# Two graph aggregations as one paired Strassen step in half PSUM banks, in a tuned two-layer GNN kernel

One core of one Trainium2 chip. The metric is the device time of the whole program in microseconds (us), the median of several runs. A profiled run also gives a span, about 1.8 us shorter than its time, and a trace.

## The reference, cut to what matters

64 graphs with 256 nodes and 512 features, everything fp32. Two layers, each followed by a residual and a layer norm:

```python
x   = jax.random.normal(..., (64, 256, 512))        # adj: (64, 256, 256), nodemask: (64, 256), all ones
# layer 0
deg = jnp.sum(adj, axis=-1, keepdims=True)
agg = jnp.einsum('bij,bjf->bif', adj, x) / jnp.maximum(deg, EPS)
out = jnp.einsum('bnf,of->bno', jnp.concatenate([x, agg], axis=2), W)
x   = layernorm(x + relu(out))
# layer 1
q, k = jnp.split(x @ Wqk, 2, axis=-1);  v = x @ Wv
agg  = jnp.einsum('bij,bjd->bid', adj, k * mask[:, :, None])
w    = inv_scale * mask * jnp.einsum('bid,bid->bi', q, agg)
x    = layernorm(x + softmax(w, axis=1)[:, :, None] * v)
```

## The kernel before

The kernel multiplies the weights first: layer 0 computes y = x W2 and then adj y; layer 1 computes x1 M with M = Wq Wk^T and takes its row-wise dot product with adj (mask x1). So each graph has two large products with weights (256 x 512 by 512 x 1024) and two aggregations (256 x 256 by 256 x 512). The large products already go by a Strassen step with seven block products (`product`); the aggregations go directly, four matmuls with 512 columns each. All accumulation is in PSUM: seven banks of 128 x 512 fp32 rotate (`bank`), and a block product often accumulates into the bank that ACT (the scalar engine) has just copied out, for example U -> copy -> U + S3\*T3 -> copy -> U + A22\*T4. I call that a *bank turn*.

```python
    def product(ps, a, b, start=True):
        for c in range(H):                                     # H = 2: two matmuls of 512 columns
            nc.tensor.matmul(ps, a[:, c, :], b[:, c, :], start=start and c == 0, stop=(c == H - 1),
                             skip_group_check=True)

    def aggregate(a, vals, t):                                 # goes
        ps = bank()
        for j in range(NT):                                    # NT = 2
            nc.tensor.matmul(ps, a[:, j, t * P:(t + 1) * P], vals[:, j, :],
                             start=(j == 0), stop=(j == NT - 1))
        return ps
    ...
    def transpose_rows(src, dst):                              # x1 -> x1T: 32x32 on DVE, the rest by 16 DMAs
        sq = pool.tile([P, P // Q, NF, NT, Q], F32, name="sq")
        for t in range(NT):
            nc.vector.transpose(sq[:, :, :, t, :].rearrange("p b c q -> p c b q"), src[:, t, :])
        to = dst.rearrange("f c (t a q) -> f (c t) a q", t=NT, q=Q)
        for a in range(P // Q):
            for b in range(P // Q):
                nc.sync.dma_start(to[b * Q:(b + 1) * Q, :, a, :], ...)
    ...
    def gather0(g):                                            # layer 0's aggregation, out of PSUM
        for t in range(NT):
            z = aggregate(adj_g, y, t)
            nc.vector.scalar_tensor_tensor(own[:, t, :], z, rdeg[:, t:t + 1], own[:, t, :],
                                           op0=OP.mult, op1=OP.add)
            nc.vector.scalar_tensor_tensor(own[:, t, :], own[:, t, :], 0.0, xg[:, t, :],
                                           op0=OP.max, op1=OP.add)
    def gather1(g):                                            # layer 1's, with a masked adjacency from GpSimd
        sums1[g] = row_sums(x1Ts.pop(g), nc.vector)
        for t in range(NT):
            nc.scalar.copy(agg[:, t, :], aggregate(adjm, x1s[g], t))
    ...
    for i in range(B + G + 2):                                 # layer 0 of graph i beside layer 1 of graph i-2
        if new: layer0_a(i)
        ... softmax of two graphs, in every second iteration ...
        if old: gather1(i - 2)
        if new: layer0_b(i)
        ...
        if old: layer1_a(i - 2)
        if new: gather0(i)
        if old: layer1_b(i - 2)
        if new: norm0(i)
        if i + 1 < B: prepare(i + 1)
```

## Time and profile before

| | before |
|---|---|
| time, median of 3 runs | 2049.61 us (2048.89 to 2050.76) |
| PE (matrix engine) busy | 2017.6 us of a span of 2047.8, 99% |
| DVE / ACT / POOL busy | 58% / 25% / 13% |
| first product of one graph to that of the next | 30.90 us, and 31.53 in graphs with a softmax |

A matmul with 512 fp32 columns is two records in the trace (the page counts x512 for the 256 matmuls of one aggregation). A line of the timeline joins like records that follow each other (x4 is one block product); its second column runs to the modelled end of the last one, so the distance between two starts is what a block product costs (1.72 us), not the duration (1.88). "[0.68 <-ACT y L205]" is idle time just before, and what ended it.

### The profile page before, as it was taken

To read this page: it belongs to the slowest core of one execution; us is meant where nothing else is said; L and a number is where in the kernel's file an instruction comes from. 1 tells how busy PE (TensorE), PEld (TensorE's weight loads), DVE (VectorE), ACT (ScalarE), POOL (GpSimd) and SP (SyncE) were. 2 spreads that over 40 slices of the span, in tenths; PEclk is the share of its full clock that TensorE was granted. 3 is DMA by queue.
4 is the path that set the end of the run, shared out by engine and by line. 5 is a ranking of instruction groups with operands and counts; after the bars stand their busy time and mean duration, and the time that the engine had idled before them with its cause. 6 is when DMAs were issued, how large, how long until landed. Compare 5 with 4: busy or idle time off the path is not lost.

```text
span 2047.8 us, 16517 instructions
## 1 busy us (share of the span) xinstructions
PE 2017.6 (99%) x4768; PEld 888.9 (43%) x4768; DVE 1188.1 (58%) x2729; ACT 521.3 (25%) x1094; POOL 273.3 (13%) x391
## 2 busy tenths in 40 slices
PE   7999999999999999999999999999999999999996
PEld 3444444444444444444444444444444444444442
DVE  3555656655556556566556565565665565655656
ACT  2222222222222222222222222222222222222122
POOL 4010111110110111111101101101111011011000
PEclk9999999999999999999999999999999999999998
DMA  7323332333232333333333323323333333223211
GB/s 244 99 70 84 91 82 75 95 77 88 82 88 79 85 91 86 81 76 94 77 90 87 91 72 86 91 85 80 77 93 82 87 90 82 67 77 77 56 37 52
DMA packets 384601, 174.22 MB, mean 85 GB/s; under 512 B 283776, under 2 KB 349440, under 8 KB 384512
## 3 DMA queue, kind: packets, MB, share of 16 engines
q1 hardware_dynamic: 382096, 167.92, 30.7%
q10 hardware_dynamic: 2144, 4.19, 0.6%
q8 instruction: 39, 0.64, 0.1%
q0 software_dynamic: 272, 1.05, 0.1%
q14 instruction: 50, 0.41, 0.1%
HBM read 105.97 MB, written 33.55 MB: 68 GB/s over the span
## 4 chain that ended last, share of the span: by engine, by line
PE 98%; DMA 1%; DVE 1%; ACT 0%; issue 0%; SPq 0%; DVEq 0%; ACTq 0%
PE mm L140 75%; PE mm L161 21%; DMA xT<-x_t 1%; DMA rows<-adj 0%; PE tp L295 0%; PE tp L281 0%; DMA wqk<-wqk_t 0%; DVE o L303 0%; DVE st L169 0%; DVE o L175 0%; DVE y L215 0%; ACT L287 0%; ACT y L205 0%; ACT rows L182 0%; DVE v L272 0%
## 5 line engine op out<-in xcount | busy, mean ns | idle before, releaser
L140 PE MATMUL mm<-w,s 128*128 128x512 f32 x1024 | 481.2, 592 | 0.0
L140 PE MATMUL mm<-t,s 128*128 128x512 f32 x1024 | 462.6, 594 | 5.1 <-ACT own L198 2.8
L140 PEld LDWEIGHTS mm<-t,s 128*128 128x128 f32 x1024 | 194.7, 190 | 250.7 <-issue 247.1
L140 PEld LDWEIGHTS mm<-w,s 128*128 128x128 f32 x1024 | 194.5, 190 | 245.0 <-issue 223.9
L188 POOL TENSOR_SCALAR adjm<-adj,mask_sb 128x256 f32<-128x256 f32 x128 | 65.7, 524 | 1483.4 <-PE mm L161 1322.5
L140 PE MATMUL mm<-w,x1T 128*128 128x512 f32 x512 | 243.7, 598 | 0.0
L140 PE MATMUL mm<-w,xT 128*128 128x512 f32 x512 | 240.6, 592 | 0.0
L161 PE MATMUL mm<-y,adj 128*128 128x512 f32 x512 | 230.4, 592 | 1.6 <-DVE y L215 1.6
L161 PE MATMUL mm<-x,adjm 128*128 128x512 f32 x512 | 230.4, 592 | 0.0
L215 DVE TENSOR_TENSOR y<-mm,y 128x512 f32<-128x512 f32 x64 | 44.3, 692 | 281.2 <-PE mm L140 281.2
L161 PEld LDWEIGHTS mm<-y,adj 128*128 128x128 f32 x512 | 97.1, 190 | 124.7 <-issue 106.9
L140 PEld LDWEIGHTS mm<-w,xT 128*128 128x128 f32 x512 | 97.5, 190 | 123.0 <-issue 118.5
L140 PEld LDWEIGHTS mm<-w,x1T 128*128 128x128 f32 x512 | 94.8, 190 | 108.6 <-issue 108.1
L161 PEld LDWEIGHTS mm<-x,adjm 128*128 128x128 f32 x512 | 94.9, 190 | 108.4 <-issue 106.7
L140 PE MATMUL mm<-t,xT 128*128 128x512 f32 x256 | 120.5, 593 | 1.4 <-ACT y L205 1.4
L140 PE MATMUL mm<-t,x1T 128*128 128x512 f32 x256 | 120.5, 593 | 0.7 <-ACT v L260 0.7
L303 DVE SCALAR_TENSOR_TENSOR o<-v,probs,x 128x512 f32<-128x512 f32 x128 | 119.0, 967 | 1.1
L182 ACT ACTIVATE rows<-rows 128x256 f32<-128x256 f32 x128 | 52.3, 409 | 257.1 <-DVE mv L170 166.2
L221 DVE SCALAR_TENSOR_TENSOR own<-mm,rdeg,own 128x512 f32<-128x512 f32 x128 | 95.0, 742 | 29.5 <-PE mm L161 29.5
L172 ACT ACTIVATE rstd<-mv,eps 128x2 f32<-128x2 f32 x128 | 37.4, 292 | 283.7 <-DVE mv L170 283.7
L257 DVE SCALAR_TENSOR_TENSOR agg<-mm,agg 128x512 f32<-128x512 f32 x64 | 44.0, 688 | 108.9 <-PE mm L140 108.8
L261 DVE TENSOR_TENSOR v<-mm,v 128x512 f32<-128x512 f32 x64 | 44.3, 691 | 90.8 <-ACT v L260 90.8
(68 smaller groups left out, 1802.8 us busy)
## 6 DMA issues: line engine op xcount, KB each, us to landing
xT<-x_t SPq DMA_DIRECT2D x64, 512.0 KB, 4.6
x<-x SPq DMA_DIRECT2D x64, 512.0 KB, 3.6
x1T<-sq SPq DMA_DIRECT2D x1024, 32.0 KB, 2.0
out<-o SPq DMA_DIRECT2D x64, 512.0 KB, 3.1
adj<-adj_t SPq DMA_DIRECT2D x64, 256.0 KB, 2.6
rows<-adj SPq DMA_DIRECT2D x64, 256.0 KB, 3.2
wqk<-wqk_t ACTq DMA_DIRECT2D x4, 512.0 KB, 11.1
w<-w_t ACTq DMA_DIRECT2D x2, 1024.0 KB, 9.1
```

Source lines behind the costliest of these rows:

```text
L140: nc.tensor.matmul(ps, a[:, c, :], b[:, c, :], start=start and c == 0, stop=(c == H - 1), skip_group_check=True)
L161: nc.tensor.matmul(ps, a[:, j, t * P:(t + 1) * P], vals[:, j, :], start=(j == 0), stop=(j == NT - 1))
L172: nc.scalar.activation(rstd, mv[:, :, 1], AF.Sqrt, bias=eps)
L182: nc.scalar.activation(r[:, t, :], r[:, t, :], AF.Copy, accum_out=deg[:, t:t + 1])
L188: nc.gpsimd.tensor_scalar(adjms[g][:, j, :], adjs[g][:, j, :], mask_sb[:, j, g:g + 1], 1.0, op0=OP.mult, op1=OP.mult)
L215: nc.vector.tensor_add(y[:, 0, :], p5, y[:, 0, :])
L221: nc.vector.scalar_tensor_tensor(own[:, t, :], z, rdeg[:, t:t + 1], own[:, t, :], op0=OP.mult, op1=OP.add)
L257: nc.vector.scalar_tensor_tensor(agg[:, 0, :], p2, 1.0, agg[:, 0, :], op0=OP.mult, op1=OP.mult, accum_out=sc[:, 0, at:at + 1])
L261: nc.vector.tensor_add(v[:, 1, :], p5, v[:, 1, :])
L303: nc.vector.scalar_tensor_tensor(o[:, t, :], v[:, t, :], p[:, t, g % G:g % G + 1], x1[:, t, :], op0=OP.mult, op1=OP.add)
```

## The change

The intent is to use seven block products in place of eight in the aggregations too. A 256 x 256 by 256 x 512 product has blocks with 256 columns only, so two aggregations share each PSUM bank: layer 0's of graph g in one half, layer 1's of graph g-1 in the other. The differences of the adjacency go to GpSimd, those of the values to DVE (the vector engine), the mask to two ACT copies. Layer 1's aggregation thereby moves one iteration earlier, and the iteration's end is interleaved: one product of layer 1, one pair of aggregation products, and so on.

```diff
-    def aggregate(a, vals, t): ...
     def prepare(g):
-        adjms[g] = ...                                          # masked adjacency, 2 x GpSimd
+        nc.gpsimd.tensor_add(sa[:, 0], a21, a22)
+        nc.gpsimd.tensor_sub(sa[:, 1], sa[:, 0], a11)
+        nc.gpsimd.tensor_sub(sa[:, 2], a11, a21)
+        nc.gpsimd.tensor_sub(sa[:, 3], a12, sa[:, 1])
+    def gather_a(g):
+        tv = pool.tile([P, 4, 2, HF], F32, name="tv", bufs=1)
+        nc.vector.tensor_sub(t1, b12, b11)
+        nc.vector.tensor_sub(t2, b22, t1)
+        nc.vector.tensor_sub(t3, b22, b12)
+        nc.vector.tensor_sub(t4, b21, t2)
+        def twice(ps, a, b, start=True):                         # HF = 256 columns each
+            for n, k in enumerate(which):
+                nc.tensor.matmul(ps[:, k * HF:(k + 1) * HF], sumsA[g - k][a], w[b][:, n, :],
+                                 start=start and n == 0, stop=True, skip_group_check=True)
+        def steps():
+            twice(u, "A11", "B11");  nc.scalar.copy(r11, of(u))
+            twice(p2, "A12", "B21"); nc.vector.tensor_add(r11, of(p2), r11)
+            yield
+            twice(p5, "S1", "T1")
+            twice(u, "S2", "T2", start=False); nc.scalar.copy(r12, of(u))
+            yield
+            twice(u, "S3", "T3", start=False); nc.scalar.copy(r22, of(u))
+            nc.vector.tensor_add(r22, of(p5), r22)
+            yield
+            twice(u, "A22", "T4", start=False); nc.scalar.copy(r21, of(u))
+            yield
+            twice(p5, "S4", "B22", start=False); nc.vector.tensor_add(r12, of(p5), r12)
+            yield
     def norm0(g):
         layer_norm(owns.pop(g), x1s[g])
+        for t in range(NT):                                      # masked x1: layer 1's half of the next step
+            nc.scalar.activation(values(g + 1)[:, 1, t, :], x1s[g][:, t, :], AF.Copy,
+                                 scale=mask_sb[:, t, g:g + 1])
-    layer1_a, layer1_b
+    def layer1_steps(g):        # the same seven products, a yield after each:
+        # A11*B11 | S1*T1 | S2*T2 | A12*B21 | S3*T3 | A22*T4 | S4*B22
     for i in range(B + G + 2):
...
-        if old: layer1_a(i - 2)
-        if new: gather0(i)
-        if old: layer1_b(i - 2)
+        z = gather_a(i) if i <= B else iter(())
+        step(l1, 2)
+        step(z); step(l1); step(z); step(l1); step(z); step(l1); step(z); step(l1); step(z)
```

Small edits come with it: Wv's load goes to another DMA queue, the buffer `sq` of the transposition is single, and the DMA scratch is smaller.

More of the change, by code (lines that the diff above doesn't have):

```diff
@@ L62, in resnorm_kernel @@
     NT, NF, NA = N // P, F // P, A // P
-    H = NF // 2
+    H, HF = NF // 2, F // 2
     assert NT == 2 and NF == 4
@@ L71, in resnorm_kernel @@
     ps_tp = ctx.enter_context(tc.tile_pool(name="ps_tp", bufs=1, space=bass.MemoryType.PSUM))
-    (xs, adjs, rows, xTs, sums0, adjms, rdegs, ys, owns, x1s, x1Ts, sums1, aggs, vs, scores, probs,
-     open0, open1) = ({} for _ in range(18))
+    (xs, adjs, rows, xTs, sums0, sumsA, rdegs, vals, owns, x1s, x1Ts, sums1, aggs, vs, scores, probs,
+     open0) = ({} for _ in range(17))
     def load(g):
@@ L100, in resnorm_kernel @@
         nc.sync.dma_start(mask_sb, mask_t)
-        nc.gpsimd.dma_start(w1[:, NF:, :], wv.rearrange("(c p) o -> p c o", p=P))
+        nc.sync.dma_start(w1[:, NF:, :], wv.rearrange("(c p) o -> p c o", p=P))
         ident = const.tile([P, P], F32, name="ident")
@@ L146, in transpose_rows @@
     def transpose_rows(src, dst):
-        sq = pool.tile([P, P // Q, NF, NT, Q], F32, name="sq")
+        sq = pool.tile([P, P // Q, NF, NT, Q], F32, name="sq", bufs=1)
         for t in range(NT):
@@ L156, in transpose_rows @@
                                   sq[a * Q:(a + 1) * Q, b].rearrange("p c t q -> p (c t) q"))
-    def aggregate(a, vals, t):
-        ps = bank()
-        for j in range(NT):
-            nc.tensor.matmul(ps, a[:, j, t * P:(t + 1) * P], vals[:, j, :],
-                             start=(j == 0), stop=(j == NT - 1))
-        return ps
     def layer_norm(src, dst):
@@ L185, in prepare @@
         nc.vector.reciprocal(rdegs[g], rdegs[g])
-        adjms[g] = pool.tile([P, NT, N], F32, name="adjm", bufs=4)
-        for j in range(NT):
-            nc.gpsimd.tensor_scalar(adjms[g][:, j, :], adjs[g][:, j, :], mask_sb[:, j, g:g + 1], 1.0,
-                                    op0=OP.mult, op1=OP.mult)
+        a, sa = adjs[g], pool.tile([P, 4, P], F32, name="sa", bufs=3)
+        a11, a21, a12, a22 = a[:, 0, :P], a[:, 0, P:], a[:, 1, :P], a[:, 1, P:]
+        nc.gpsimd.tensor_add(sa[:, 0], a21, a22)
+        nc.gpsimd.tensor_sub(sa[:, 1], sa[:, 0], a11)
+        nc.gpsimd.tensor_sub(sa[:, 2], a11, a21)
+        nc.gpsimd.tensor_sub(sa[:, 3], a12, sa[:, 1])
+        sumsA[g] = {"A11": a11, "A12": a12, "A22": a22, "S1": sa[:, 0], "S2": sa[:, 1], "S3": sa[:, 2],
+                    "S4": sa[:, 3]}
         sums0[g] = row_sums(xTs.pop(g), nc.gpsimd)
@@ L194, in layer0_a @@
         own = owns[g] = pool.tile([P, NT, F], F32, name="own")
-        y = ys[g] = pool.tile([P, NT, F], F32, name="y")
+        y = values(g)[:, 0]
         u, p5, p2 = bank(), bank(), bank()
@@ L209, in layer0_b @@
     def layer0_b(g):
-        s, w, own, y = sums0.pop(g), W0, owns[g], ys[g]
+        s, w, own, y = sums0.pop(g), W0, owns[g], values(g)[:, 0]
         u, p5 = open0.pop(g)
@@ L215, in layer0_b, with values, of @@
         nc.vector.tensor_add(y[:, 0, :], p5, y[:, 0, :])
-    def gather0(g):
-        own, y, adj_g, rdeg, xg = owns[g], ys.pop(g), adjs.pop(g), rdegs.pop(g), xs.pop(g)
+    def values(g):
+        if g not in vals:
+            vals[g] = pool.tile([P, 2, NT, F], F32, name="vals")
+        return vals[g]
+    def gather_a(g):
+        val = vals.pop(g)
+        which = [k for k in range(2) if 0 <= g - k < B]
+        k0, k1 = which[0], which[-1] + 1
+        b11, b12, b21, b22 = (val[:, k0:k1, t, h * HF:(h + 1) * HF] for t in range(NT) for h in range(2))
+        tv = pool.tile([P, 4, 2, HF], F32, name="tv", bufs=1)
+        t1, t2, t3, t4 = (tv[:, k, k0:k1, :] for k in range(4))
+        nc.vector.tensor_sub(t1, b12, b11)
+        nc.vector.tensor_sub(t2, b22, t1)
+        nc.vector.tensor_sub(t3, b22, b12)
+        nc.vector.tensor_sub(t4, b21, t2)
+        w = {"B11": b11, "B21": b21, "B22": b22, "T1": t1, "T2": t2, "T3": t3, "T4": t4}
+        zr = aggs[g] = pool.tile([P, 2, NT, F], F32, name="zr")
+        r11, r12, r21, r22 = (zr[:, k0:k1, t, h * HF:(h + 1) * HF] for t in range(NT) for h in range(2))
+        def twice(ps, a, b, start=True):
+            for n, k in enumerate(which):
+                nc.tensor.matmul(ps[:, k * HF:(k + 1) * HF], sumsA[g - k][a], w[b][:, n, :],
+                                 start=start and n == 0, stop=True, skip_group_check=True)
+        def of(ps):
+            return ps.rearrange("p (k f) -> p k f", k=2)[:, k0:k1, :]
+        def steps():
+            u, p5, p2 = bank(), bank(), bank()
+            twice(u, "A11", "B11")
+            nc.scalar.copy(r11, of(u))
+            twice(p2, "A12", "B21")
+            nc.vector.tensor_add(r11, of(p2), r11)
+            yield
+            twice(p5, "S1", "T1")
+            twice(u, "S2", "T2", start=False)
+            nc.scalar.copy(r12, of(u))
+            yield
+            twice(u, "S3", "T3", start=False)
+            nc.scalar.copy(r22, of(u))
+            nc.vector.tensor_add(r22, of(p5), r22)
+            yield
+            twice(u, "A22", "T4", start=False)
+            nc.scalar.copy(r21, of(u))
+            yield
+            twice(p5, "S4", "B22", start=False)
+            nc.vector.tensor_add(r12, of(p5), r12)
+            yield
+        return steps()
@@ L219, in gather0, with combine0 @@
+    def combine0(g):
+        own, z, rdeg, xg = owns[g], aggs[g][:, 0], rdegs.pop(g), xs.pop(g)
         for t in range(NT):
-            z = aggregate(adj_g, y, t)
-            nc.vector.scalar_tensor_tensor(own[:, t, :], z, rdeg[:, t:t + 1], own[:, t, :],
+            nc.vector.scalar_tensor_tensor(own[:, t, :], z[:, t, :], rdeg[:, t:t + 1], own[:, t, :],
                                            op0=OP.mult, op1=OP.add)
@@ L228, in norm0, with turn @@
         layer_norm(owns.pop(g), x1s[g])
+        for t in range(NT):
+            nc.scalar.activation(values(g + 1)[:, 1, t, :], x1s[g][:, t, :], AF.Copy,
+                                 scale=mask_sb[:, t, g:g + 1])
         x1Ts[g] = pool.tile([P, NF, N], F32, name="x1T")
         transpose_rows(x1s[g], x1Ts[g])
-    def gather1(g):
+    def turn(g):
         sums1[g] = row_sums(x1Ts.pop(g), nc.vector)
-        agg = aggs[g] = pool.tile([P, NT, F], F32, name="agg")
-        adjm = adjms.pop(g)
-        for t in range(NT):
-            nc.scalar.copy(agg[:, t, :], aggregate(adjm, x1s[g], t))
-    def layer1_a(g):
+    def layer1_steps(g):
         if g % G == 0:
@@ L244, in layer1_a, with dot @@
         at = g % G
-        s, w, agg = sums1[g], W1, aggs[g]
+        s, w, agg = sums1.pop(g), W1, aggs.pop(g + 1)[:, 1]
         v = vs[g] = late.tile([P, NT, F], F32, name="v", bufs=G + 2)
         q = pool.tile([P, F], F32, name="q")
-        u, p5, p2 = bank(), bank(), bank()
+        def dot(a, t, to):
+            nc.vector.scalar_tensor_tensor(q, a, 1.0, agg[:, t, :], op0=OP.mult, op1=OP.mult, accum_out=to)
+        u = bank()
         product(u, s["A11"], w["B11"])
         nc.scalar.copy(q, u)
+        dot(q, 0, part[:, at:at + 1])
+        yield
+        p5 = bank()
         product(p5, s["S1"], w["T1"])
-        nc.vector.scalar_tensor_tensor(q, q, 1.0, agg[:, 0, :], op0=OP.mult, op1=OP.mult,
-                                       accum_out=part[:, at:at + 1])
+        yield
         product(u, s["S2"], w["T2"], start=False)
         nc.scalar.copy(v[:, 0, :], u)
+        yield
+        p2 = bank()
         product(p2, s["A12"], w["B21"])
-        nc.vector.scalar_tensor_tensor(agg[:, 0, :], p2, 1.0, agg[:, 0, :], op0=OP.mult, op1=OP.mult,
-                                       accum_out=sc[:, 0, at:at + 1])
+        dot(p2, 0, sc[:, 0, at:at + 1])
+        yield
         product(u, s["S3"], w["T3"], start=False)
@@ L261, in layer1_a @@
         nc.vector.tensor_add(v[:, 1, :], p5, v[:, 1, :])
-        open1[g] = u, p5
-    def layer1_b(g):
-        s, w, agg, v = sums1.pop(g), W1, aggs.pop(g), vs[g]
-        sc, at = scores[g // G][0], g % G
-        u, p5 = open1.pop(g)
+        yield
         product(u, s["A22"], w["T4"], start=False)
-        nc.vector.scalar_tensor_tensor(agg[:, 1, :], u, 1.0, agg[:, 1, :], op0=OP.mult, op1=OP.mult,
-                                       accum_out=sc[:, 1, at:at + 1])
+        dot(u, 1, sc[:, 1, at:at + 1])
+        yield
         product(p5, s["S4"], w["B22"], start=False)
         nc.vector.tensor_add(v[:, 0, :], p5, v[:, 0, :])
+        yield
     def softmax_rows(k):
@@ L311, in resnorm_kernel, with step @@
     W1 = weight_sums(w1, "t1_")
+    def step(gen, n=1):
+        for _ in range(n):
+            next(gen, None)
     for i in range(B + G + 2):
-        new, old = i < B, 0 <= i - 2 < B
+        new = i < B
         if i + 2 < B:
@@ L321, in resnorm_kernel @@
             e = softmax_rows(k)
-        if old:
-            gather1(i - 2)
+        if 0 <= i - 2 < B:
+            turn(i - 2)
+        l1 = layer1_steps(i - 2) if 0 <= i - 2 < B else iter(())
+        step(l1)
         if new:
@@ L329, in resnorm_kernel @@
             finish(i - 2 - G)
-        if old:
-            layer1_a(i - 2)
+        z = gather_a(i) if i <= B else iter(())
+        step(l1, 2)
+        step(z)
+        step(l1)
+        step(z)
+        step(l1)
+        step(z)
+        step(l1)
+        step(z)
+        step(l1)
+        step(z)
         if new:
-            gather0(i)
-        if old:
-            layer1_b(i - 2)
-        if new:
+            combine0(i)
             norm0(i)
@@ L347 @@
     B, N, F = x.shape
-    nc = bacc.Bacc("TRN2", target_bir_lowering=False, num_devices=1)
+    nc = bacc.Bacc("TRN2", target_bir_lowering=False, num_devices=1, dynamic_dma_scratch_size=1024)
     given = {
```

## The prediction

> **What bounds the kernel now.** I read the page's busy line first, then the matrix engine's waits over the whole run, then one stretch of the steady state by windows, then the timeline for the distance between matmuls.
>
> ```profile
> PE 2017.6 (99%) x4768; PEld 888.9 (43%) x4768; DVE 1188.1 (58%) x2729; ACT 521.3 (25%) x1094; POOL 273.3 (13%) x391
> ...
> PE mm L140 75%; PE mm L161 21%; DMA xT<-x_t 1%; DMA rows<-adj 0%; PE tp L295 0%; PE tp L281 0%; DMA wqk<-wqk_t 0%; DVE o L303 0%; DVE st L169 0%; DVE o L175 0%; DVE y L215 0%; ACT L287 0%; ACT y L205 0%; ACT rows L182 0%; DVE v L272 0%
> ...
> L161 PE MATMUL mm<-y,adj 128*128 128x512 f32 x512 | 230.4, 592 | 1.6 <-DVE y L215 1.6
> L161 PE MATMUL mm<-x,adjm 128*128 128x512 f32 x512 | 230.4, 592 | 0.0
> ```
>
> The second line is the chain that ended last: 96% of it is matmuls, 21% the aggregations (line 161) that the change rewrites. A busy PE alone proves little, so its waits:
>
> ```profile
> PE mm L111 <- DMA wqk<-wqk_t: 6.1, 1, 6.1
> PE tp L295 <- DVE e L289: 3.6, 1, 3.6
> PE mm L140 <- ACT own L198: 2.8, 1, 2.8
> PE mm L140 <- DVE t L120: 2.3, 1, 2.3
> PE mm L161 <- DVE y L215: 1.6, 2, 0.8
> PE mm L140 <- ACT y L205: 1.4, 2, 0.7
> PE mm L140 <- ACT v L260: 0.7, 1, 0.7
> ```
>
> These are all of them: 18.5 us, each at most twice, so they belong to the start and the end. By windows, the 1600 us from 200 to 1800 have 1600.00 us of PE at a clock of 1.00. In the steady state the time is the count of matmul records times their pitch. The pitch is in the timeline (columns: start, duration):
>
> ```profile
> 969.27 1.88 PE L140 MATMUL mm<-w,xT 128*128 128x512 f32 x4
> 970.99 3.60 PE L140 MATMUL mm<-t,s 128*128 128x512 f32 x8
> ...
> 996.74 1.88 PE L140 MATMUL mm<-t,x1T 128*128 128x512 f32 x4
> ```
>
> From 969.27 to 996.74 lie 64 records in 27.47 us: 0.4292 us each[...]. The page counts 512 records for 256 matmuls of the program (four per graph), so a program matmul with 512 columns is two records, 0.858 us[...]. A graph has 36 such matmuls (14 for each Strassen product, 8 for the aggregations): 72 records, 30.9 us. That fits two graphs in 62.43 us, with a softmax of some 0.6 us in every second one.
>
> [...]This trace's weight-load records last 190 ns, but two loads without a long matmul to hide behind stand 0.11 us apart:
>
> ```profile
> 1008.75 0.38 PE L281 MATMUL tp<-ident,scores 128*2 128x128 f32 x2
> 1008.76 0.08 PEld L281 LDWEIGHTS tp<-ident,scores 128*2 128x2 f32 x1 [0.34 <-issue]
> 1008.87 0.30 PEld L161 LDWEIGHTS mm<-x,adjm 128*128 128x128 f32 x2
> ...
> 1008.97 3.60 PE L161 MATMUL mm<-x,adjm 128*128 128x512 f32 x8
> ```
>
> Two transpose records of 128 output columns take from 1008.75 to 1008.97, 0.11 each[...], and the aggregation follows at once, though its weights began to load only 0.10 us earlier. [...]the two-input line 303, which runs beside POOL's sums, takes 967 ns, line 223 of the same form 694.
>
> **The change part by part.**
> PE: out go 8 matmuls of 512 columns per graph, 16 records of 0.4292: 6.87 us. In come seven block products for two graphs, each of 256 columns into its half of a bank: 14 matmuls, 28 records.[...] The gain is 0.825 us per graph, times 64: **52.8 us**. The first and the last step, with one graph only, are two halves and change nothing in the count.[...]
> DVE: four differences from SBUF and three additions from PSUM of 512 elements are new; line 221 reads SBUF in place of PSUM. In the timeline independent operations of that size start 0.60 to 0.66 apart: 7 x 0.65 = 4.5 us per graph, on top of 1188/64 = 18.6. That is 23.1 of some 30.4 us, 76%: not a bound by the sum.
> ACT: four copies of 0.58 for two, and two masked copies[...]: +2.5 on 8.1 us, 35%.
> POOL: the masked adjacency (2 x 0.52) goes, four differences of 128 x 128 come (estimate 0.4 each, from 0.73 for 256 columns): even.
> DMA: the same bytes; Wv's load moves to another queue, before it is needed.
>
> **What could turn into a wait.** The scheduled order of PE in the new kernel is: five products of layer 0, the first of layer 1, two of layer 0, then products of layer 1 (1.72 us each) in turn with pairs of aggregation products (0.86). I laid the measured durations on it by hand, PE running without a gap, and asked for each semaphore whether its producer is done.
> The tightest is PSUM reuse. Layer 1's S3*T3 is copied out by ACT and the next product accumulates in the same bank; now only one aggregation pair (0.864) lies between them, before it was four matmuls (3.4). The start of this trace shows such a turn bare:
>
> ```profile
> 36.34 1.88 PE L140 MATMUL mm<-w,s 128*128 128x512 f32 x4
> 38.26 0.58 ACT L205 COPY y<-mm 128x512 f32<-128x512 f32 x1 [0.58 <-PE mm L140]
> 38.89 1.98 PE L140 MATMUL mm<-t,xT 128*128 128x512 f32 x4 [0.68 <-ACT y L205]
> ```
>
> PE's last column went in at 36.34 + 4 x 0.4292 = 38.06 and PE went on at 38.89: 0.83 us. It fits into 0.864 by 0.03. I allow 0.03 a graph: 2 us.
> The differences T1 to T4 wait behind the last layer norm on DVE in softmax iterations, with POOL's sums beside them; there T2 is done about 20.3 us into the iteration, and PE asks for it at 22.1. The layer norm's end, now after the last aggregation product, gives the masked x1 at about 8.6 of the next iteration; it is asked for at 17. The softmax weights' transposes have 1.1 us to spare. None of these should show.
> The start is even: in the first two graphs no layer 1 fills the waits, but the scheduler puts the next graph's first product between; I add 0.5.
> The end is not: x1 of the last graph now comes some 6 us later (the aggregation ends the iteration, it used to precede the last two products). Its transposition through 16 DMAs, issued in 10.4 us (timeline before), ends near 21.8 us after the previous iteration, while PE has work until about 17, waits for masks and T1 (1.5) included. So +6.3 us.
> Sum: 2049.6 - 52.8 + 2 + 0.5 + 6.3 = **2005.6**, say 2005: 2.2% faster.
>
> **The rivals.**
> (a) The short record costs more than its columns: weights or instruction supply pace it. For it: weight-load records of 190 ns leave 26 ns in 216, and no matmul with 128 stationary columns and fewer than 512 output columns is in this trace. Against it: the 0.11 us spacing above. If a record took 230 ns, 1792 of them would add 25 us: 2030, within 2%. At 245 the gain is gone.
> (b) DVE or ACT become the bound within the iteration although their sums are not[...]. For it: DVE at 76%, two finishing layer norms moved into every second iteration, POOL's contention. Against: 0.9 us or more of slack at each of the points but the bank turn. If I am off by 1 us at one point, 0.3 to 1 us in every second graph: 10 to 30 us, 2015 to 2035.
> (c) Everything hidden and the end cheaper than I think: 1997 to 2000.
>
> **Range and chances.** The gain of 52.8 is firm if the pitch is; 2% is 41.0, so some 12 us of new waits are allowed and I count 8.8. Errors are likelier upward. Range 1998 to 2016; faster by over 2%: 0.66, within 2%: 0.32, slower: 0.02.
>
> **What would show it.** Right: records of 256 columns start 0.216 apart; two graphs pass in 62.43 - 1.65 = 60.8 us; PE's waits in the steady state come to under 5 us, and a wait for the transposed x1 of about 4.5 appears at the end; DVE 72 to 78% busy. Wrong: a pitch above 0.22 (rival a); a wait that recurs 32 or 64 times, on T (DVE), on a copy of layer 1's bank (ACT), or on layer 0's bank behind the masked copies (rival b).

It had put a record with 256 columns at 215.8 ns, so the 28 new records of a graph at 6.04 us, against 6.87 for the 16 old ones: 0.825 us a graph and 52.8 in all. With that the sum came to 2049.6 - 52.8 + 2 + 0.5 + 6.3 = 2005.6 us. The pitch was measured afterwards, in the changed kernel: 215.8 ns. From the trace before alone an estimate is possible: 0.11 us for a record of 128 columns and 0.4292 for one of 512, on a straight line, give 0.216 for 256. One masked copy on ACT in the changed kernel took 0.71 us on average (line 281).

## More of the kernel before

Near the start there are a product behind a wait of 2.82 us and a bank turn. Near the end there is another bank turn (2012.60), and the last graph's transposed x1 is asked for; it is there already, so there is no wait in front of the last line:

```profile
31.14 3.65 PE L140 MATMUL mm<-t,s 128*128 128x512 f32 x4 [2.82 <-ACT own L198]
...
56.34 1.98 PE L140 MATMUL mm<-t,xT 128*128 128x512 f32 x4 [0.68 <-ACT y L205]
...
2012.60 1.96 PE L140 MATMUL mm<-t,x1T 128*128 128x512 f32 x4
...
2016.12 2.74 PE L161 MATMUL mm<-x,adjm 128*128 128x512 f32 x6
2018.69 1.88 PE L140 MATMUL mm<-w,x1T 128*128 128x512 f32 x4
```

## The result, and the profile after

| | before | after |
|---|---|---|
| time, median | 2049.3 us (4 runs) | **2012.62 us** (4 runs, 2011.77 to 2013.55) |
| ratio | 1 | 0.982 (95%: 0.9803 to 0.9837) |

A ratio is the mean time of one kernel's runs over the mean of the other's in the same rounds, so it is not quite the ratio of the medians. The gain is 36.7 us, 1.8%. That is within the predicted range (1998 to 2016) but 7.6 us above the predicted 2005, and on the other side of the 2% line from the class that I had held likeliest.

The page of the kernel after, with the lines that answer to those of before (L142 is `product`, L240 is `twice`):

```profile
PE 1973.9 (98%) x5536; PEld 1030.4 (51%) x5536; DVE 1523.6 (76%) x3184; ACT 673.2 (33%) x1354; POOL 419.0 (21%) x518
...
L142 PE MATMUL mm<-w,x1T 128*128 128x512 f32 x512 | 242.5, 596 | 4.1 <-DMA x1T<-sq 4.1
...
L240 PE MATMUL mm<-tv,sa 128*128 128x256 f32 x768 | 187.1, 379 | 0.0
```

PE lost 43.7 us of busy time and is still the bound; DVE rose from 58 to 76%. All of PE's waits:

```profile
PE mm L113 <- DMA wqk<-wqk_t: 6.2, 1, 6.2
PE mm L142 <- DMA x1T<-sq: 4.1, 1, 4.1
PE mm L142 <- ACT own L197: 3.8, 1, 3.8
PE tp L349 <- DVE e L343: 3.6, 1, 3.6
PE mm L142 <- ACT vals L204: 3.0, 3, 2.1
PE mm L240 <- DVE vals L214: 1.6, 2, 0.8
PE mm L142 <- ACT v L311: 0.7, 1, 0.7
PE mm L142 <- ACT v L318: 0.7, 1, 0.7
PE mm L142 <- ACT q L304: 0.6, 1, 0.6
PE mm L142 <- DVE t L122: 0.4, 1, 0.4
```

No wait recurs from graph to graph, and by windows PE is again busy for 1600.00 us of the 1600 from 200 to 1800. Only the wait for x1T is new in kind. But this view does not tell everything, as the steady state shows. The timeline of PE, with the start of graphs' layer 0 (`mm<-w,xT` before a `mm<-t,s` x8) in the last three lines:

```profile
1002.74 1.89 PE L240 MATMUL mm<-tv,sa 128*128 128x256 f32 x8
1004.47 1.88 PE L142 MATMUL mm<-w,s 128*128 128x512 f32 x4
1006.18 1.03 PE L240 MATMUL mm<-tv,sa 128*128 128x256 f32 x4
1007.05 1.96 PE L142 MATMUL mm<-t,x1T 128*128 128x512 f32 x4
1008.84 1.03 PE L240 MATMUL mm<-tv,adj 128*128 128x256 f32 x4
...
1012.28 1.88 PE L142 MATMUL mm<-w,xT 128*128 128x512 f32 x4
...
1042.44 1.88 PE L142 MATMUL mm<-w,xT 128*128 128x512 f32 x4
...
1073.22 1.88 PE L142 MATMUL mm<-w,xT 128*128 128x512 f32 x4
```

Eight records with 256 columns take from 1002.74 to 1004.47, 0.216 each: the pitch is as predicted (over all steady runs of eight, 1.727 us, 215.8 ns each). Two graphs take 60.94 us (1012.28 to 1073.22) where I had said 60.8. The missing 0.14 to 0.16 is in the fourth line: A22\*T4 of layer 1 takes 1.80 us to the next start and not 1.72, in every graph. It is the product behind the bank turn that I had called the tightest. ACT's and the weight loads' rows of the same moment in the timeline:

```profile
1006.38 0.58 ACT L318 COPY v<-mm 128x512 f32<-128x512 f32 x1 [1.13 <-PE mm L142]
...
1007.02 0.30 PEld L142 LDWEIGHTS mm<-t,x1T 128*128 128x128 f32 x2 [0.21 <-ACT v L318]
```

The copy ends at 1006.96, and only then, at 1007.02, the first weights of the next product load: 0.03 us before the matmul at 1007.05. The matmul is not late, so no wait is counted, but its weights are, and the product is 0.08 us longer.

The span in three sections, from the starts of the first product of graph 3 and of graph 63 in the traces (the end runs to the start of the last matmul; some 12 us of layer norm and output follow in every kernel):

| | start, to graph 3 | middle, 60 graphs | end, from graph 63 |
|---|---|---|---|
| before | 95.26 | 1872.88 | 67.63 |
| after | 98.18 | 1828.21 | 71.92 |
| difference | +2.92 | -44.67 | +4.29 |

The middle is 60 x 0.745 us: 0.825 saved by the records, 0.079 given back at the bank turn. Of the start, 1.37 us is work moved there (layer 1's aggregation comes a graph earlier) and 1.55 are waits. In the end there are 4.67 us fewer records (that work, and the Strassen gain), so 8.96 us are waits or slow records.

The start: T4 of graph 1 waits 2.10 us where the kernel before waited 0.68 for the same bank turn.

```profile
54.86 1.33 ACT L281 ACTIVATE vals<-x,mask_sb 128x512 f32<-128x512 f32 x2 [0.81 <-DVE x L170]
56.10 0.56 ACT L204 COPY vals<-mm 128x512 f32<-128x512 f32 x1
...
56.72 1.98 PE L142 MATMUL mm<-t,xT 128*128 128x512 f32 x4 [2.10 <-ACT vals L204]
```

On ACT the bank copy (L204) stands behind the new masked copies (L281), and these had waited for the layer norm.

The end, on PE and then by windows (columns: stretch; its length; busy time and count of PE, PEld, DVE, ACT, POOL; PEclk; DMA share; GB/s):

```profile
1973.57 0.59 PE L240 MATMUL mm<-vals,sa 128*128 128x256 f32 x2
1978.28 3.75 PE L142 MATMUL mm<-w,x1T 128*128 128x512 f32 x4 [4.11 <-DMA x1T<-sq]
1981.83 4.72 PE L142 MATMUL mm<-t,s 128*128 128x512 f32 x8
1986.38 1.88 PE L142 MATMUL mm<-w,x1T 128*128 128x512 f32 x4
```

```profile
1978.28:1981.83 3.55, 3.55 (x5) 1.48 (x5) 1.50 (x4) 0.00 (x0) 0.00 (x0) 0.50 0.67 246
1981.83:1986.38 4.55, 4.55 (x9) 1.96 (x8) 0.70 (x2) 0.58 (x1) 0.00 (x0) 0.75 0.00 0
```

The wait for the last x1T was predicted. What follows was not: the granted clock is 0.50, then 0.75 on average. One block product takes 3.55 us and not 1.72, the next two 4.55 and not 3.43: 2.95 us lost to the wait's aftermath. PE's last column before the gap went in at 1974.00 (two records of 0.2158 after 1973.57). By windows the clock was 1.00 up to 1977.24, still inside the gap, 0.50 for the 6.83 us from there to 1984.07, and 1.00 behind that, up to 1994.2. It had fallen once before in this trace: behind a wait of 3.77 us that ended at 30.50 it was 0.50 for the 3.42 us from 31.65 to 35.07. The kernel before shows the same thing near its start: the product at 31.14, behind its wait of 2.82 us, took 3.44 us and not 1.72, at a clock of 0.51:

```profile
31.14:34.58 3.44, 3.44 (x4) 1.38 (x5) 3.44 (x5) 1.61 (x8) 3.44 (x2) 0.51 0.50 152
```

Extra waits predicted and found, in us: start 0.5 and 1.55; bank turn 2 and 4.75; end 6.3 and 8.96; sum 8.8 and 15.3. With the records' 52.8, 52.8 - 15.3 = 37.5 us, and the two spans differ by 37.6 (2047.8 and 2010.2).

### The profile page after: what moved, and what is told of

Read it like the earlier page. It is cut to its first block, busy times and chain, and to the rows that moved or that the text cites. A ratio compares the mean times of both kernels' runs of the same rounds, so it can differ in the third digit from the quotient of the medians.

```text
span 2010.2 us, 19340 instructions
## 1 busy us (share of the span) xinstructions
PE 1973.9 (98%) x5536; PEld 1030.4 (51%) x5536; DVE 1523.6 (76%) x3184; ACT 673.2 (33%) x1354; POOL 419.0 (21%) x518
## 4 chain that ended last, share of the span: by engine, by line
PE 95%; DVE 1%; ACT 1%; SPq 0%; issue 0%; DMA 0%; DVEq 0%; ACTq 0%
PE mm L142 75%; PE mm L240 19%; SPq L157 0%; PE tp L349 0%; PE tp L335 0%; DVE st L164 0%; DVE o L357 0%; DVE own L272 0%; ACT L341 0%; ACT vals L281 0%; DMA x1T<-sq 0%; ACT rows L177 0%; DVE o L170 0%; DVE own L274 0%; DVE v L325 0%
## 5 line engine op out<-in xcount | busy, mean ns | idle before, releaser
L142 PE MATMUL mm<-w,s 128*128 128x512 f32 x1024 | 481.3, 592 | 0.7 <-ACT v L311 0.7
L142 PE MATMUL mm<-t,s 128*128 128x512 f32 x1024 | 466.2, 597 | 4.8 <-ACT own L197 3.8
L142 PEld LDWEIGHTS mm<-t,s 128*128 128x128 f32 x1024 | 192.3, 190 | 236.7 <-issue 215.5
L142 PEld LDWEIGHTS mm<-w,s 128*128 128x128 f32 x1024 | 194.4, 190 | 192.8 <-issue 163.2
L142 PE MATMUL mm<-w,x1T 128*128 128x512 f32 x512 | 242.5, 596 | 4.1 <-DMA x1T<-sq 4.1
L142 PE MATMUL mm<-w,xT 128*128 128x512 f32 x512 | 242.0, 594 | 0.0
L183 POOL TENSOR_TENSOR sa<-adj 128x128 f32<-128x128 f32 x64 | 47.1, 736 | 781.0 <-PE mm L240 774.3
L134 POOL TENSOR_TENSOR s<-xT 128x256 f32<-128x256 f32 x64 | 47.7, 745 | 703.6 <-PE mm L142 685.8
L240 PE MATMUL mm<-tv,sa 128*128 128x256 f32 x768 | 187.1, 379 | 0.0
L240 PEld LDWEIGHTS mm<-tv,sa 128*128 128x128 f32 x768 | 145.8, 190 | 74.6 <-issue 59.6
L142 PEld LDWEIGHTS mm<-w,xT 128*128 128x128 f32 x512 | 97.9, 191 | 95.8 <-issue 92.4
L272 DVE SCALAR_TENSOR_TENSOR own<-zr,rdeg,own 128x512 f32<-128x512 f32 x128 | 107.6, 841 | 44.4 <-ACT zr L262 44.4
L142 PEld LDWEIGHTS mm<-w,x1T 128*128 128x128 f32 x512 | 95.3, 191 | 86.1 <-issue 74.6
L300 DVE SCALAR_TENSOR_TENSOR q<-mm,zr 128x512 f32<-128x512 f32 x128 | 87.7, 685 | 66.1 <-PE mm L142 66.1
L311 ACT COPY v<-mm 128x512 f32<-128x512 f32 x64 | 37.4, 585 | 299.0 <-PE mm L142 299.0
L142 PE MATMUL mm<-t,x1T 128*128 128x512 f32 x256 | 125.5, 612 | 0.7 <-ACT v L318 0.7
L142 PE MATMUL mm<-t,xT 128*128 128x512 f32 x256 | 120.6, 593 | 3.0 <-ACT vals L204 3.0
L240 PE MATMUL mm<-vals,adj 128*128 128x256 f32 x512 | 121.3, 379 | 1.6 <-DVE vals L214 1.6
L240 PEld LDWEIGHTS mm<-vals,adj 128*128 128x128 f32 x512 | 97.1, 190 | 43.2 <-issue 21.5
L214 DVE TENSOR_TENSOR vals<-mm,vals 128x512 f32<-128x512 f32 x64 | 44.3, 692 | 91.8 <-PE mm L142 91.8
```

The costliest lines, as they stand in the source:

```text
L134: eng.tensor_add(s1, a21, a22)
L183: nc.gpsimd.tensor_add(sa[:, 0], a21, a22)
L214: nc.vector.tensor_add(y[:, 0, :], p5, y[:, 0, :])
L240: nc.tensor.matmul(ps[:, k * HF:(k + 1) * HF], sumsA[g - k][a], w[b][:, n, :], start=start and n == 0, stop=True, skip_group_check=True)
L272: nc.vector.scalar_tensor_tensor(own[:, t, :], z[:, t, :], rdeg[:, t:t + 1], own[:, t, :], op0=OP.mult, op1=OP.add)
L300: nc.vector.scalar_tensor_tensor(q, a, 1.0, agg[:, t, :], op0=OP.mult, op1=OP.mult, accum_out=to)
```

## The experiments

My theory: the records give what was predicted; 4.7 us are lost at layer 1's bank turn in the steady state and about 7 us at the last x1T (wait and half clock). The rivals: (b) DVE or ACT are so near to bounding the iteration that freed time comes back elsewhere; (d) the small edits or the pairing in half banks cost something by themselves; (e) the half clock is not a consequence of the idle time. All kernels gave correct results. Runs e1, e3, e4 and e8 shared a chip and runs of the kernel before (median 2049.47), and e2, e5, e6 and e7 others (2049.5).

| run | time, us | ratio to before | start | middle | end |
|---|---|---|---|---|---|
| before | 2049.3 | 1 | 95.26 | 1872.88 | 67.63 |
| after | 2012.62 | 0.982 | 98.18 | 1828.21 | 71.92 |
| e1_reorder | 2005.48 | 0.9787 | 98.05 | 1823.48 | 69.92 |
| e3_fill | 2011.50 | 0.9815 | 99.33 | 1828.20 | 70.17 |
| e8_pe_turn | 2006.66 | 0.9790 | 99.25 | 1828.21 | 65.58 |
| e2_two_queues | 2006.11 | 0.9791 | 98.21 | 1828.21 | 65.79 |
| e4_twice_T | 2045.43 | 0.9978 | 103.26 | 1860.94 | 69.02 |
| e5_classical | 2055.90 | 1.0033 | 101.03 | 1875.28 | 66.83 |
| e7_side_edits | 2048.96 | 0.9997 | 94.57 | 1872.88 | 67.64 |
| e6_both | 2001.18 | 0.9764 | 99.94 | 1823.48 | 64.78 |

The sections are of the one profiled run of each. The middle repeats to 0.01 us between kernels that share its code. The start does not: for kernels with the code of the changed one there it lies between 98.05 and 99.94, so differences below 2 us are read from middle and end alone. The clock differs there too. In the changed kernel it stood at half for 3.42 us (31.65 to 35.07, a mean of 0.83 over 30 to 40 us). In e3 and e8 the means are 0.98 and 0.97 over 20 to 30 us and 0.68 and 0.69 over 30 to 40, which makes 6.8 us at half in each, by my estimate. In e6, with 0.83 over 30 to 40, it fell once more: 0.94 over 40 to 60 and 0.99 over 60 to 100, where the changed kernel has 1.00 (both kernels have a longest wait for line 204's bank copy of 2.1 us).

### e1_reorder: more work between the copy and the turn

```diff
     # layer1_steps
-        p2 = bank(); product(p2, s["A12"], w["B21"]); dot(p2, 0, sc[:, 0, at:at + 1])
-        yield
         product(u, s["S3"], w["T3"], start=False)
         ...
         product(u, s["A22"], w["T4"], start=False)
         dot(u, 1, sc[:, 1, at:at + 1])
         yield
+        p2 = bank(); product(p2, s["A12"], w["B21"]); dot(p2, 0, sc[:, 0, at:at + 1])
+        yield
```

A12\*B21, which has a bank of its own, moves behind A22\*T4; so S3\*T3 and A22\*T4 now have eight short records between them (1.73 us) and not four (0.86).

> Only the order of layer 1's products changes: S3*T3, then two aggregation pairs, then A22*T4, and A12*B21 moves behind it, so that 1.73 us of other matmuls (before 0.86) lie between the two that share a PSUM bank. Theory (the copy out of the bank ends 0.03 to 0.1 us too late, so the weight load of A22*T4 cannot be hidden): in the changed kernel A22*T4 takes 1.796 us to the next product in place of 1.717, in every graph; that 0.079 goes, two graphs take 60.78 us in place of 60.94, and the time falls by 5 us, from 2012.6 to about 2007.6. Rival (the 0.08 us is a cost of going from 256 columns back to 512, or of that operand): it stays with A22*T4 wherever it stands, and the time stays within 1 us.

Measured: 2005.48 us (2005.0 to 2006.57), ratio 0.9787 (0.9774 to 0.9801), 7.1 us under the changed kernel. Its timeline:

```profile
1944.03 1.89 PE L240 MATMUL mm<-tv,sa 128*128 128x256 f32 x8
1945.76 1.88 PE L142 MATMUL mm<-t,x1T 128*128 128x512 f32 x4
```

A22\*T4 (the second line) lasts 1.88 and not 1.96, 1.72 us to the next start, two graphs 60.78, and the middle is 4.73 us shorter: the bank turn is shown to be the loss of the steady state, all of it. The end gained 2.0 us as well: one turn fewer waits there (0.68), the softmax's transposition waits 3.3 and not 3.6, and after the same wait for x1T (4.04 us) the half clock lasted about 3.4 us and not 6.83, so the two products after it took 3.44 and not 4.55. I take that part for timing and not for the edit's doing, but no run shows what decides it. By windows the clock here was 1.00 up to 1973.36, where PE went on, 0.51 over the 3.48 us of the first product and 1.00 over the next 3.44; in the changed kernel PE went on at 1978.28, 1.04 us after the clock had fallen.

### e3_fill: keep PE busy during the last wait, with matmuls that nobody reads

```diff
+        if i == B:
+            fill = bank()
+            for _ in range(4):
+                nc.tensor.matmul(fill, aggs[B][:, 1, 1, :P], W1["B22"][:, 0, :], start=True, stop=True)
         if new:
             combine0(i)
```

> Four matmuls whose result nobody uses are put on PE before the last graph's layer 1, into the 4.1 us in which PE waits for the transposed x1. They do not make the data come sooner. Theory[...]: the wait shrinks to about 0.7 us but the first product of the last graph starts at the same time after its predecessor as before, at a clock of 1.00 in place of 0.50; its first two products take 1.72 us each, not 3.5 and 2.8: the time falls by 2.5 to 3 us, to about 2010. Rival (the two products are slow because they wait for row sums and DMA bytes): no change, 2012 to 2013.

(What it rested on is the end of the changed kernel: a wait of 4.11 us, and then a clock of 0.50 over one product and 0.75 over the next two.)

Measured: 2011.50 us (2011.3 to 2011.69), ratio 0.9815: 1.1 us under the changed kernel, less than the 2.5 to 3 that I had expected.

```profile
1974.72 0.59 PE L240 MATMUL mm<-vals,sa 128*128 128x256 f32 x2
1975.15 3.60 PE L404 MATMUL mm<-w,zr 128*128 128x512 f32 x8
1980.59 1.95 PE L142 MATMUL mm<-w,x1T 128*128 128x512 f32 x4 [1.84 <-issue]
1982.38 3.60 PE L142 MATMUL mm<-t,s 128*128 128x512 f32 x8
```

It went as thought: behind an idle stretch of 1.84 us the products run at full speed, 1.79 and 3.43 us, and by windows the clock is 1.00 from 1970 to 1987. So the half clock goes with the longer idle stretch, and rival (e) falls. The size was not as thought: from the end of the last aggregation product to the first product with x1T this kernel needs 5.44 us (1975.15 to 1980.59), the changed kernel 4.28 (1974.00 to 1978.28). In this run the sixteen DMAs took 11.47 us to issue and not 10.42; whether the fill caused that or it was chance, one profile doesn't tell. That 1.05 us, and a start that was 1.15 us longer, account for the shortfall.

### e8_pe_turn: the last graph's x1 transposed by PE, not by 16 DMAs

```diff
+    def turn_last(g):
+        for t in range(NT):
+            ps = bank()
+            for c in range(NF):
+                nc.tensor.transpose(ps[:, c * P:(c + 1) * P], x1s[g][:, t, c * P:(c + 1) * P], ident)
+            nc.vector.tensor_copy(x1Ts[g][:, :, t * P:(t + 1) * P], ps.rearrange("p (c n) -> p c n", c=NF))
     # norm0: transpose_rows only if g < B - 1;  main loop, before the last step(l1), step(z):
+        if i == B:
+            turn_last(B - 1)
```

> The last graph's x1 alone is transposed on PE (8 transposes, copied out by DVE) in place of VectorE's 32x32 blocks and 16 DMAs. Theory (the end's loss is a wait of 4.1 us for the 16 DMAs, and the granted clock that falls to 0.50 after it costs another 2.5 to 3): the wait for x1T and the half clock go, 8 transposes of 0.22 us come: the time falls by about 5 us, to 2007.5. Rival (the end is bound by the layer norm and the masked copies of the last graph, and the DMAs were hidden behind that): less than 1.5 us.

Measured: 2006.66 us (2005.73 to 2006.92), ratio 0.9790 (0.9777 to 0.9804), 6.0 us under the changed kernel.

```profile
1972.93 1.04 PE L291 MATMUL mm<-ident,x 128*128 128x128 f32 x8
1973.80 1.88 PE L142 MATMUL mm<-w,s 128*128 128x512 f32 x4
1975.52 0.59 PE L240 MATMUL mm<-vals,sa 128*128 128x256 f32 x2
1975.95 1.88 PE L142 MATMUL mm<-w,x1T 128*128 128x512 f32 x4
```

Eight transposes cost 0.87 us of PE (0.11 each, half of what I had expected), the product follows the aggregation without a gap, and the end is 6.34 us shorter: 4.1 of wait and 2.95 of half clock, less the transposes' 0.87, make 6.2. The middle is unchanged.

### e2_two_queues: the same 16 DMAs from two queues

```diff
-    def transpose_rows(src, dst):
+    def transpose_rows(src, dst, last=False):
...
-                nc.sync.dma_start(to[b * Q:(b + 1) * Q, :, a, :],
+                eng = nc.scalar if last and b % 2 else nc.sync
+                eng.dma_start(to[b * Q:(b + 1) * Q, :, a, :],
```

> For the last graph only, half of the 16 transposing DMAs are issued from the ACT queue. Theory (the end waits because one queue takes 10.4 us to issue them, 0.65 each): issued in some 5.2 us, x1T is there about 5 us sooner, but ACT's copies of the last aggregation stand behind its 8 issues; the wait of 4.1 us for x1T goes, about 2 us of waits for ACT come, the half clock does not: the time falls by 3 to 5 us, to 2008 to 2010. Rival (the transfers themselves or the completion take the time): the 16 land no sooner, and the time stays at 2012 or rises.

Measured: 2006.11 us (2005.75 to 2007.57), ratio 0.9791 (0.9778 to 0.9805), 6.5 us under the changed kernel. The timeline of its end, the issue of the DMAs on both queues first:

```profile
1966.21 5.19 SPq L158 DMA_DIRECT2D x1T<-sq  x8
...
1966.38 5.37 ACTq L158 DMA_DIRECT2D x1T<-sq  x8
...
1975.43 0.70 PE L241 MATMUL mm<-vals,sa 128*128 128x256 f32 x2
1975.97 1.02 PE L142 MATMUL mm<-w,x1T 128*128 128x512 f32 x2
1976.83 3.60 PE L142 MATMUL mm<-t,s 128*128 128x512 f32 x8
```

Two queues issue their eight DMAs side by side in 5.2 and 5.4 us, one queue issued its sixteen in 10.42. There is no wait for x1T and no half clock, and the gain is more than the 3 to 5 us expected. So it was the serial issue on one queue, not the transfers themselves, that made x1T late. In its place the waits show 0.5 us for a copy of the aggregation's bank (line 256): ACT, busy issuing until 1971.75, is late with its copies. PE does not notice more than that.

### e4_twice_T: the four new DVE differences computed twice

```diff
-        nc.vector.tensor_sub(t1, b12, b11)
-        nc.vector.tensor_sub(t2, b22, t1)
-        nc.vector.tensor_sub(t3, b22, b12)
-        nc.vector.tensor_sub(t4, b21, t2)
+        for _ in range(2):
+            nc.vector.tensor_sub(t1, b12, b11)
+            nc.vector.tensor_sub(t2, b22, t1)
+            nc.vector.tensor_sub(t3, b22, b12)
+            nc.vector.tensor_sub(t4, b21, t2)
```

This tests rival (b): how far is DVE from bounding the iteration?

> The four differences T1 to T4 are computed twice, so that DVE has 2.6 us more per graph (4.5 where POOL runs beside it) and is about 84% busy. Theory (DVE's part of the change is hidden, with 2.4 us of slack before PE asks for T2 in the graphs with a softmax and 3.8 in the others): nothing or at most 1 us in every second graph, 2012 to 2035. Rival (DVE is nearly the bound and the added 4.7 us per graph already show): its whole 2.6 us per graph comes through, 2150 or more.

Measured: 2045.43 us (2042.78 to 2046.88), ratio 0.9978, so 32.8 us slower than the changed kernel. Its waits and its timeline:

```profile
PE mm L241 <- DVE tv L231: 16.2, 33, 1.8
...
PE mm L241 <- DVE tv L232: 4.9, 30, 0.2
```

```profile
1023.90 1.10 PE L241 MATMUL mm<-tv,sa 128*128 128x256 f32 x4 [0.31 <-DVE tv L231]
1025.16 1.10 PE L241 MATMUL mm<-tv,sa 128*128 128x256 f32 x4 [0.16 <-DVE tv L232]
```

Both lines of the timeline are in a graph with a softmax. Such graphs took 31.88 us on average and not 30.78, the others 30.16 as in the changed kernel. So four more operations (some 2.5 us: their starts are 0.57 to 0.73 apart where POOL is idle) vanish in every second graph, and cost 1.09 us in the others. The step per graph was about what I had written, but the total that I put beside it was mis-multiplied: 1 us in every second graph is 32 us, which is 2045 and not the 2012 to 2035 of the text. The changed kernel has slack on DVE in graphs with a softmax, some 1.4 us by this sum (2.5 less 1.09), and in its own trace T2 is done 2.2 us (1.8 to 2.4) before PE starts on it, 3.7 in the other graphs. T never makes PE wait. Rival (b) is false for this kernel, though not far away.

### e5_classical: paired in half banks, but eight block products

```diff
+            for out, rows_, cols in ((r11, ("A11", "A12"), ("B11", "B21")), (r12, ("A11", "A12"), ("B12", "B22")),
+                                     (r22, ("A21", "A22"), ("B12", "B22")), (r21, ("A21", "A22"), ("B11", "B21"))):
+                ps = bank()
+                twice(ps, rows_[0], cols[0])
+                twice(ps, rows_[1], cols[1], start=False)
+                nc.scalar.copy(out, of(ps))
+                yield
```

No sums of the adjacency, no differences of the values, no accumulation over a copied bank in the aggregation; everything else is the changed kernel.

> The aggregations stay paired, half a bank each, with 256 columns, but as the 8 block products of the plain form: no differences of the adjacency or of the values, no additions after. It separates the eighth product from the way the pair is built. Theory (the time is the count of records times their pitch): 32 records of 0.2158 per graph, 6.91 us, 0.86 above the Strassen step and 0.04 above before; no stall at A22*T4, since 1.73 us lie between: two graphs in 62.5 us; with the end's wait 2056 to 2063, so 45 to 50 us above the changed kernel and slower than before by up to 0.7%. Rival (pairing or the interleaving itself gives or takes something in the steady state): two graphs differ from 62.5 us by over 0.2.

Measured: 2055.90 us (2055.84 to 2056.79), ratio 1.0033 (1.002 to 1.0045), just under the 2056 to 2063 expected. Two graphs take 62.51 us.

```profile
1937.86 1.89 PE L228 MATMUL mm<-vals,adj 128*128 128x256 f32 x8
1939.59 1.88 PE L142 MATMUL mm<-t,x1T 128*128 128x512 f32 x4
1941.30 1.89 PE L228 MATMUL mm<-vals,adj 128*128 128x256 f32 x8
```

Per graph it is 31.255 us: 0.040 more than before, as 32 x 0.2158 (6.906) against 16 x 0.4292 (6.867) says; and 0.785 more than the changed kernel, as four records (0.863) less the bank turn's 0.079 say. (Here eight records lie in the turn, and A22\*T4 takes 1.71.) So in the steady state pairing in half banks costs nothing but these 0.040 us, and the whole gain of the change is the eighth of the block products that Strassen's step leaves out. The profiled spans of e5 and before differ by 7.2 us: 2.4 of it in the middle, 5.8 at the start, to which a whole aggregation (3.45) is moved, and the end gives back only 0.8. I read that as the price of the shifted aggregation at the edges and not of the half banks; no run shows it apart.

### e7_side_edits: the kernel before with the three small edits alone

```diff
-        nc.gpsimd.dma_start(w1[:, NF:, :], wv.rearrange("(c p) o -> p c o", p=P))
+        nc.sync.dma_start(w1[:, NF:, :], wv.rearrange("(c p) o -> p c o", p=P))
-        sq = pool.tile([P, P // Q, NF, NT, Q], F32, name="sq")
+        sq = pool.tile([P, P // Q, NF, NT, Q], F32, name="sq", bufs=1)
-    nc = bacc.Bacc("TRN2", target_bir_lowering=False, num_devices=1)
+    nc = bacc.Bacc("TRN2", target_bir_lowering=False, num_devices=1, dynamic_dma_scratch_size=1024)
```

> The kernel before with only the change's side edits: Wv loaded on the sync queue in place of GpSimd's, one buffer for the transposition's squares in place of two, the smaller scratch for dynamic DMA. Theory (they make room and cost nothing): 2049.5 within 1.5 us, two graphs in 62.43. Rival (they have a part in the start's 1.5 us): 1.5 to 3 us more, all of it before graph 3.

Measured: 2048.96 us (2048.71 to 2049.11), ratio 0.9997 (0.9985 to 1.001): the same. With e5, rival (d) falls: neither the edits nor, in the steady state, the pairing cost anything that matters.

### e6_both: e1 and e8 together

The edit is the sum of the two diffs.

> The two changes that worked alone, together: layer 1's products reordered (alone 2005.5, of which 61 x 0.079 = 4.8 us in the steady state) and the last graph's x1 transposed on PE (alone 2006.7). Theory (they touch different places and add up): 2012.6 - 4.8 - 6.5 = 2001, 2.3 to 2.4% below before; two graphs in 60.78 us, no wait for x1T, no half clock between graph 3 and the final softmax. Rival (the reorder already took part of the end's loss, 7.1 us in all for 4.8 in the steady state): 2002 to 2004.

Measured: **2001.18 us** (1999.74 to 2001.83), ratio 0.9764 (0.975 to 0.9777): the fastest of all, 2.4% under the kernel before, and the one whose interval lies wholly beyond 2%. The middle is that of e1, the end is shorter still than that of e8. In middle and end it gains 11.87 us on the changed kernel (4.73 + 7.14), and e1 and e8 apart 13.07 (6.73 + 6.34): the half clock that was some 3.4 us shorter in e1 is gone altogether in e8 (1.00 from 1975 to 1992), so that part cannot be had twice.

## Why the prediction was right or wrong

- **The records (52.8 us): right.** Pitch 215.8 ns where 215.8 was predicted; the weight-load records of 190 ns did not pace it (rival a). The middle gives 60 x 0.824 once the bank turn is taken out.
- **The bank turn (0.03 a graph, 2 us): the place right, the size wrong.** It is 0.079 a graph, 4.75 us in sixty graphs; e1 gave all of it back. The step that failed is "0.83 us. It fits into 0.864 by 0.03". I measured the turn at the start of the matmul (38.89) and overlooked the same row's duration, 1.98 where a product without a turn has 1.88: the first weights load only after the copy, and that lengthens the product by another 0.10. So the turn needs about 0.93 us, 0.07 more than it has. The case itself stood in the before kernel's trace: its last graph's A22\*T4 (2012.60) comes two records, 0.86 us, after S3\*T3, lasts 1.96 and takes 1.80 to the next start.
- **DVE and ACT (rival b): right.** DVE 76% as worked out, ACT 33% (35%), no recurring wait. T2 is done 2.2 us before PE starts on it in softmax graphs, where I had 1.8.
- **POOL ("even"): wrong, without effect.** It went from 273 to 419 us. The differences took 0.45 to 0.78 us each on average, not 0.4, and the longer feature sums rose too (one from 725 to 1116 ns, while DVE's busy share rose from 58 to 76%). Off the path.
- **The start (0.5): too small.** 1.55 us of waits, nearly all of it one: ACT's bank copy behind the masked copies, 1.4 us more than before. I had looked at the scheduled order of PE, and for the start not at ACT's. The other 1.37 us of the longer start is work that the end no longer has, so it costs nothing by itself. No experiment took this wait away.
- **The end (6.3): the waits right, their aftermath missing.** Waits that the kernel before does not have there sum to 5.38 us (4.11 for x1T where I had 4.5 to 4.8, 0.68 and 0.59 behind ACT), and about 0.6 more is left by subtraction; weights exposed behind the two ACT waits (0.1 each, as above) can be part of it. The 2.95 us that failed is the half clock after the gap. The prediction treated a wait as costing its own length; e3 and e8 show that this one also slowed the next three products. This too could have been read beforehand, from the before kernel's product at 31.14: 3.65 us in the duration column, where 1.88 is usual.
- **The chances.** Of the 12 us of new waits that the 2% line allowed I had counted 8.8, with errors "likelier upward"; 15.3 came. The three terms missed by +1.05, +2.75 and +2.66, in sum 6.5; the remaining 1.1 of the 7.6 us lies in rounding 2005.6 down and between the profiled run (37.6 gained) and the medians (36.7), less 0.3 because I had started from 2049.6 and not 2049.3. Of the 7.6, 5.4 come from two things that the profile shows in one row and one column: the duration of the product behind a wait, and PEclk.

## What to carry to other kernels

Size a bank turn from the end of the last product to the *second* start after it, so that the exposed weight load (0.08 to 0.10 us here) is in it, and put the product with a bank of its own into the tightest turn rather than a loose one. A wait on PE of 4.11 us cost 7.1 here, 2.95 of it by the half clock behind it, and one of 1.84 (e3) only itself. Behind one of 2.10 the clock stayed at 1.00 in the changed kernel, while in e6, with a wait as long, the means over 40 to 100 us say some 1.6 us lost, an estimate; what decides this was not shown. So moving work towards the end of a pipelined loop needs the clock in its sum, and a serial queue of small DMAs that was hidden in the loop must be shortened for the last step (two queues were enough here: 5.2 and 5.4 us of issue side by side, against 10.42 on one). Where the time was records times pitch, the gain was that of the records left out (0.824 us a graph of 0.825), and the work of prediction is in the edges.

## More that these traces show

- 28 short records a graph, each with its own weight load, ran at a pitch of 215.8 ns (changed kernel, all steady runs of eight). One matmul of the program is two records there, 0.4292 us each with 512 columns and 0.2158 with 256. The weight-load records last 186 to 190 ns (`--tile sa`), and did not bound a record of 216.
- A weight load that could not be pulled ahead because its product waited cost 0.08 us per turn with the matmul itself on time (A22\*T4 of the changed kernel, 1.80 us and not 1.72; e1 takes it away), and 0.10 with the matmul late (1.98 and not 1.88, at 38.89 in the kernel before).
- The granted clock behind waits of PE: 2.82 us in the kernel before (it ended at 31.14), 0.50 for 3.4 us from 31.24; 3.77 in the changed kernel (30.50), 0.50 for 3.42 from 31.65; 4.04 in e1 (1973.36), 0.51 over the next 3.48; 4.11 in the changed kernel (1978.28), 0.50 for 6.83 from 1977.24, still inside the wait; 1.84 in e3 (1980.59) and 2.10 in the changed kernel (56.72), 1.00 throughout. What sets the length of the half clock no run shows.
- GpSimd's 128 x 256 difference went from 725 to 1116 ns on average as DVE's share rose from 58 to 76%, and its 128 x 128 differences spread from 446 ns to 1.4 us in the changed kernel. On DVE, two operations of line 303 of the kernel before took 2.40 us with POOL busy beside them for 2.26 (at 954.41), and 1.38 with POOL idle (at 958.69).
- Sixteen DMAs of 32 KB took 10.42 us to issue on one queue, 0.65 each, where a median of 2.0 us passed from issue to landing, and two queues with eight each took 5.2 and 5.4 us side by side (e2).
